# A Mamba and mixture-of-experts kernel: a planner with other durations, scans by quarter, and convolutions as diagonal products

## The chip, the cores and the metric

The kernel runs on one core of one Trainium2 chip, as one launch. The metric is device time in microseconds of that core. A core has five engines that run their own instruction lists and wait for each other through semaphores: TensorE (PE, matrix products into PSUM), VectorE (DVE), ScalarE (ACT), GpSimd (POOL) and SyncE (SP, which here issues DMAs). Everything is float32.

## The reference

Input is `x` of 4 x 256 x 64 x 64: four sequences of 4,096 tokens with 256 channels. Two layers follow, and behind the second a mixture of experts.

Layer 0 is a Mamba block. It projects the tokens, normalises them, projects to 512 + 512 channels, sends the first half through a causal convolution over 4 tokens and a silu, and then through a selective scan with 16 states for each of the 512 channels:

```
xc = sum((xp[:, k:k + L, :] * conv_w[:, k] for k in range(K))) + conv_b
xm = silu(xc)
dt = softplus(dbl[..., :16] @ dt_w.T + dt_b)        # per token and channel
dA = exp(dt_l[..., None] * A)                       # per token, channel, state
h  = dA * h + (dt_l * x_l)[..., None] * B_l[:, None, :]
y  = einsum('bdn,bn->bd', h, C_l)
```

Layer 1 is a Mamba-2 block: a projection, a convolution over 4 tokens on 640 channels (512 for x, 64 for B, 64 for C), a silu, and a scan with one decay per token and head (8 heads of 64 channels, 64 states), with normalisations around it. The experts: each token goes to the best of 8 experts (256 to 1024 to 256 with relu), up to a capacity of 2,560 tokens each, and its result is scaled by the router's probability and added.

## The kernel before, in words

Three phases run one after the other: `mixers` (both layers), `experts`, and `turn` (the transposition of the output). Only `mixers` is touched by the change.

**Chunks and stages.** `mixers` cuts the 4 x 4,096 tokens into 64 chunks of T = 256 tokens. A chunk passes the stages `front0` (layer 0's projections and convolution, L719), `mid0` (dt and u = dt times x, written to DRAM and read back in another layout), `scan` (L831), `tail0`, `front1` (layer 1's projections and convolution), `ssd` (layer 1's scan in matrix form) and `back1` (router and the scatter of rows to the experts). The stages of several chunks run at the same time.

**The scan.** A chunk's scan has 16 units: j (four groups of 128 channels) times f (four groups of states). A tile of 128 partitions by 1,024 elements holds 4 blocks of 256 tokens (32 channels times 4 states on the partitions, four channel groups in the free dimension). In a unit, ACT computes the decays `da` (four exponentials of 255 elements with a scale per partition), DVE multiplies `ub = u * B` into PSUM and runs one `tensor_tensor_scan` over all 1,024 elements, `h = da * h + ub` (L880), POOL multiplies `p = h * C`, and PE adds up the states of `p` with `sum4` into `py`. The first element of each block of `da` is zero, so that the one scan starts each block anew. What comes from the chunk before is put into `ub`'s first elements: POOL and ACT compute `e0 = exp(dt * A) * hlast` once per j (three small instructions), and DVE adds it to four elements per unit (`ub<-ub,e`, the fix-up). `hlast` is the last column of h, copied by ACT. The `da` tiles are three fixed ones.

**The convolutions.** `front0` and `front1` write the pre-convolution values into `raw` (128 x 4 x 259, three tokens of halo in front; one buffer for both layers). `to_taps` (L684) writes it to DRAM, and `tapped` (L690) reads it back for each j with four DMAs, one for each tap, each shifted by a token, so that the partitions hold 4 taps x 32 channels. `convolve` (L700) makes four products with 32 output rows each, whose weights `taps_m` and `taps_x` (L524) are 128 x 32: PE adds up the four taps. ACT adds the bias. The B and C channels of layer 1 (`rbc`) already use four products with diagonal 128 x 128 weights, straight from SBUF.

**The order of the work.** Nothing in `mixers` is issued at once. Each operation goes into a `Plan` with its engine, an estimated duration (`mm`, `transpose`, `act`, `copy`, `dve`, `gps`, `dma`, from L219), its dependencies and a slot: `at` (L712) sets the slot to the chunk's number times 16 plus a stage offset (FRONT0, MID0, TAIL, SSD, BACK) plus, before, an entry of the table SHIFT for the n-th call. `order` (L284) then plays the engines through: whenever an engine is free, it takes the ready operation with the lowest slot that has room in its tile rings, where a value reaches another engine SIGNAL = 0.15 us late. The starts of this play give the order in which the instructions are written out; on the chip each engine runs its list in that order. All planned operations carry the line L378, where `issue` emits them; they are told apart by their tiles. A product `p` is marked `ride`: the planner starts it beside a scan, since DVE's scan (one input in PSUM) leaves free what POOL and DVE's operations with two SBUF inputs share, and ties it behind the DVE operation in front of the scan.

Of the kernel before, what the change touches and what calls it, by code (L numbers as in the profile page):

```python
# [20 lines left out]
P = 128  # L21
T = 256
# [21 lines left out]
TAIL, SSD, BACK = 18, 29, 37  # L44
AHEAD = 4

SHIFT = {
    1: -2.3, 4: 1.4, 5: 0.2, 6: -1.3, 7: -0.3, 8: -0.3, 9: -0.3, 10: -0.3, 11: -0.3, 12: -0.3, 14: -0.3, 15: -0.3,
    16: -0.3, 17: -0.3, 18: -0.3, 19: -0.3, 20: -0.3, 21: -0.3, 22: -0.3, 23: -0.3, 24: -0.3, 25: -0.3, 26: -3.3,
    27: -2.2, 28: 0.2, 29: -0.1, 30: -2.2, 31: -2.2, 32: -2.2, 33: -2.2, 34: -2.2, 35: -2.2, 36: -2.2, 37: 1.2,  # L50
    38: 0.5, 39: -2.2, 40: -2.1, 41: -2.2, 42: -2.7, 43: -2.2, 44: -2.2, 45: -6.0, 46: -2.2, 47: -2.2, 48: -2.2,
    49: -2.2, 50: -2.2, 51: -2.2, 52: -9.4, 53: -2.2, 54: -1.4, 55: -2.2, 56: -2.2, 57: -2.2, 58: -2.2, 59: -2.2,
    60: -4.7, 61: -2.2, 62: -2.2, 63: -2.2, 64: -2.2, 65: -2.2, 66: -2.2, 67: -2.7, 68: -2.2, 69: -2.2, 70: -2.2,
    71: -0.1, 72: -2.2, 73: -2.2, 74: -2.2, 75: -5.9, 76: -4.8, 77: -2.2, 78: -2.2, 79: -2.7, 80: -2.2, 81: -2.2,
    82: -2.2, 83: -2.2, 84: -2.2, 85: -5.2, 86: -2.2, 87: -2.2, 88: -2.2, 89: -2.2, 90: -2.2, 91: -1.4, 92: -2.2,
    93: -2.2, 94: -2.2, 95: -2.7, 96: -2.2, 97: -2.2, 98: -2.2, 99: -2.2, 100: -2.2, 101: -2.2, 102: -2.2,
    103: -2.2, 104: -2.2, 105: -2.2, 106: -2.3, 107: -4.0, 108: -2.0, 109: -2.2, 110: -2.2, 111: -2.2, 112: -2.2,
    113: -1.8, 114: -1.3, 115: 0.9, 116: -0.3, 117: 1.8, 118: -0.3, 119: 0.1, 120: -0.3, 121: -0.3, 123: -0.3,
    124: -0.3, 125: -0.3, 126: 0.6, 127: -1.2, 128: -0.3, 129: -0.3, 130: 0.3, 131: 0.4, 132: -1.4, 133: -0.3,
    134: -0.3, 135: -0.3, 136: 1.6, 137: -0.3, 140: 0.6,  # L60
}
# [88 lines left out]
class Plan:  # L150
# [6 lines left out]
    SIGNAL = 0.15  # L157
# [61 lines left out]
    def mm(self, out, left, right, **kw):  # L219
        rows, n = out.shape[0], self.width(right)  # L220
        w = max(0.24, n / 550) if rows > 64 else max(0.16, n / 900) if rows > 32 else max(0.15, n / 1500)
        self.note("PE", w, self.nc.tensor.matmul, (out, left, right), kw, (out,), (left, right), join=out.root)

    def transpose(self, out, src, ident):
        w = 0.08 + 0.1 * src.shape[0] / P
        self.note("PE", w, self.nc.tensor.transpose, (out, src, ident), {}, (out,), (src,), join=out.root)

    def act(self, out, src, func, **kw):
        w = 0.2 + self.width(out) / 1200
        self.note("ACT", w, self.nc.scalar.activation, (out, src, func), kw, (out,), (src, *kw.values()))  # L230

    def copy(self, out, src):
        self.note("ACT", 0.2 + self.width(out) / 1200, self.nc.scalar.copy, (out, src), {}, (out,), (src,))
# [7 lines left out]
    def dve(self, name, *args, **kw):  # L241
        out, *rest = (*args, *kw.values())
        tensors = [a for a in rest if isinstance(a, Part) or hasattr(a, "ap")]
        n = max(self.width(a) for a in (out, *tensors))
        port = len([a for a in tensors if self.on_sbuf(a) and self.width(a) > 1]) > 1
        if name == "tensor_tensor_scan":
            n, port = 2 * n, False
        op = self.note("DVE", 0.14 + n / 960, getattr(self.nc.vector, name), args, kw, (out,), rest, port=port)
        op.scan = name == "tensor_tensor_scan"
        if op.scan:  # L250
            self.scans.append(op)

# [3 lines left out]
    def gps(self, name, *args, ride=False, **kw):  # L256
        w = 0.3 + self.width(args[0]) * 2.02e-3
        f = getattr(self.nc.gpsimd, name)
        self.note("POOL", w, f, args, kw, (args[0],), args[1:], port=True, ride=ride)
# [7 lines left out]
    def scatter(self, out, rows, src, bound):  # L267


        def f(out, rows, src):  # L270
            return self.nc.gpsimd.indirect_dma_start(
                out=out,
                out_offset=bass.IndirectOffsetOnAxis(ap=rows, axis=0),
                in_=src,
                in_offset=None,
                bounds_check=bound,
                oob_is_err=False,
            )

        self.note("POOL", 1.8, f, (out, rows, src), {}, (out,), (rows, src), lag=4.0)  # L280
# [3 lines left out]
    def order(self):  # L284
# [16 lines left out]
        for op in self.ops:  # L301
            if not op.missing:
                heappush(waiting[op.engine], (0.0, op.seq, op))
        done = 0
        scan = before = last = shared = None

        def room(op, now):
            for root in op.roots:
                if not root.begun:
                    ring, queue = rings.setdefault(root.ring, []), queues[root.ring]  # L310
                    ring[:] = [o for o in ring if o.left or o.until + self.SIGNAL > now]
# [6 lines left out]
        while done < len(self.ops):  # L318
# [6 lines left out]
            for e in engines:  # L325
# [3 lines left out]
                if free[e] > now:  # L329
                    continue  # L330
# [17 lines left out]
                heappush(events, free[e])  # L348
                if op.port:
                    port[e] = free[e]  # L350
# [7 lines left out]
                for root in op.roots:  # L358
                    root.left -= 1
                    root.until = max(root.until, op.end)  # L360
                    if not root.left:
                        heappush(events, root.until + self.SIGNAL)
                for u in op.users:
                    u.missing -= 1
                    late = op.end if u.engine == e and not op.lag else op.end + self.SIGNAL
# [23 lines left out]
def tile_conv_attn_hybrid(ctx: ExitStack, tc: tile.TileContext, a: dict, out: bass.AP, cap: int, st: int):  # L389
# [41 lines left out]
    def mixers(es):  # L431
# [92 lines left out]
        def taps(scales, name):  # L524

            t = wp.tile([P, NG, R], F32, name=name, tag=name)
            for g in range(NG):
                nc.gpsimd.tensor_scalar(t[:, g], sum4, scales[:, g : g + 1], None, ALU.mult)
            return t

        taps_m = taps(m_cw, "taps_m")
        taps_x = taps(s_cw, "taps_x")

# [118 lines left out]
        def silus(*tiles, gates=0):  # L652
# [5 lines left out]
            r.acts(sum(0.2 + Plan.width(t) / 1200 for t in tiles) / len(calls) + 2.6 / len(calls), calls)  # L658
# [25 lines left out]
        def to_taps(raw, tag):  # L684

            d = scratch([NG, R, TAPS - 1 + T], tag)
            r.dma("SP", spread_rows(d), raw)
            return d

        def tapped(d, j):  # L690
            t = work([P, SQ, T], "raw4", 3)
            for k in range(TAPS):
                r.dma(
                    "SP",
                    t[k * R : (k + 1) * R],
                    d[j * SQ : (j + 1) * SQ, :, k : k + T].rearrange("g c l -> c g l"),
                )
            return t

        def convolve(raw4, weights, j, dst, bias, get):  # L700
            pi = get(T)
            for i in range(SQ):
                r.mm(pi[i * R : (i + 1) * R], weights[:, j * SQ + i], raw4[:, i], start=True, stop=True)
            r.act(dst, pi, AF.Identity, bias=bias[:, j : j + 1])
# [14 lines left out]
        def front0(k_):  # L719
# [28 lines left out]
            for half in range(2):  # L748
# [13 lines left out]
                if half == 0:  # L762
                    keep(raw, "raw0")
                    d = to_taps(raw, "raw0_d")
            for j in range(KD):
                k_.at(FRONT0 + 5 + j)
                part = tapped(d, j)
                k_.at(FRONT0 + 7 + j)
                convolve(part, taps_m, j, pre0[:, KC + KD + j], m_cb, bank_a)
# [51 lines left out]
        da_bufs = []  # L821
        for i in range(3):
            t = wp.tile([P, SQ, T], F32, name=f"da{i}", tag=f"da{i}")
            nc.gpsimd.memset(t[:, :, 0:1], 0.0)
            da_bufs.append(t)
        turn = iter(range(10**9))

        def decay_tile():
            return r.tile(lambda: da_bufs[next(turn) % len(da_bufs)], [P, SQ, T], "da", len(da_bufs))

        def scan(k_):  # L831
# [10 lines left out]
            for j in range(KD):  # L842
# [17 lines left out]
                k_.at(j * SQ - 1)  # L860
                if later:

                    e0 = work([P, SQ, SQ], "e0", 2)
                    r.gps("tensor_tensor", e0, neg_a0[:, sl], dt4[:, :, 0:1].to_broadcast([P, SQ, SQ]), ALU.mult)
                    r.act(e0, e0, AF.Exp)
                    r.gps("tensor_tensor", e0, e0, k_.prev.hlast[:, sl], ALU.mult)
                for f in range(SQ):
# [3 lines left out]
                    da = decay_tile()  # L871
                    for q in range(SQ):
                        r.act(da[:, q, 1:], dt4[:, q, 1:], AF.Exp, scale=neg_a0[:, j * SQ + q, f : f + 1])
# [3 lines left out]
                    if later:  # L877
                        r.tt(ub[:, :, 0], ub[:, :, 0], e0[:, :, f], ALU.add)
                    h = work([P, SQ, T], "h", 3)
                    r.dve("tensor_tensor_scan", h.flat(), da.flat(), ub.flat(), 0.0, ALU.mult, ALU.add)  # L880
# [50 lines left out]
        def front1(k_):  # L931
# [56 lines left out]
            d = to_taps(raw, "raw1_d")  # L988
# [46 lines left out]
            for j in range(KD):  # L1035
                k_.at(TAIL + 6 + j)
                part = tapped(d, j)
                k_.at(TAIL + 7 + j)
                convolve(part, taps_x, j, pre1[:, KD + j], s_cb, bank_b)
# [402 lines left out]
def layouts(i):  # L1442
# [14 lines left out]
    def by_tap(w):  # L1457

        return np.asarray(w).reshape(NG, R, TAPS).transpose(2, 1, 0).reshape(P, NG)
# [73 lines left out]
```

## Time and profile before

| | us |
|---|---|
| median of three runs | 6952.74 (6948.43 to 6954.37) |
| the profiled execution | 6966.12 |
| its span, first to last instruction | 6964.3 |
| first scan starts, last scan starts | 109.4, 5725.2 |
| DVE busy | 5670.3 (81%) |
| PE busy | 6084.7 (87%) |
| ACT busy | 4892.5 (70%) |
| POOL busy | 3431.0 (49%) |

The mean granted PE clock is 0.906 of full speed. In the page's rows of slices each digit stands for one fortieth of the span and gives tenths of busy time; PEclk is the granted clock in tenths. A row of groups reads: line, engine, operation, output<-inputs, shapes, count, busy time, mean ns of one, and the idle time of the engine in front of it with what ended it. PE shows each float32 product as two records. A row of the timeline reads: start, duration, engine, line, operation, tiles, shapes, count. DVE and PE take up an instruction before the one in front of it has ended, so that starts, and not durations, tell what an instruction costs in a dense sequence. A row of the table of stretches gives the length, then busy time and count of PE, weight loads, DVE, ACT and POOL, the granted clock, the DMA share and GB/s.

### The profile page before, as it was taken

The numbers are of one execution on the slowest core, as the hardware profiler recorded it, in microseconds if no ns is written. First come the engines' busy times: TensorE is split into PE (matmuls) and PEld (weight loads), VectorE is DVE, ScalarE is ACT, GpSimd is POOL, SyncE is SP. The second block draws the span as 40 slices with busy tenths as digits, with TensorE's granted clock in tenths as the row PEclk, the third lists the DMA queues.
The fourth block names the chain that finished last, engine by engine and source line by source line (L and its number), as shares of the span: only waits on it lengthen the run. The fifth ranks groups of instructions, "written<-read, shape, count | busy, mean of one in ns | idle before, by whom it ended". The sixth has DMA issues, their size and how long they took to land. (4 is left out here: it accounts for less than half of the span.)

```text
span 6964.3 us, 114017 instructions
## 1 busy us (share of the span) xinstructions
PE 6084.7 (87%) x37672; PEld 4128.5 (59%) x37672; DVE 5670.3 (81%) x7646; ACT 4892.5 (70%) x12007; POOL 3431.0 (49%) x2632
## 2 busy tenths in 40 slices
PE   5788888888888888888888888888888877999996
PEld 3455555555555555555555555555555546888886
DVE  4899999999999999999999999999999983434443
ACT  4778888888887778788887777878777863333332
POOL 3455555555555555555555555555555552333331
PEclk7899999999888988998898888989888888999998
DMA  6966667666666666666666666666666633555556
GB/s 178 255 172 178 181 178 182 178 178 178 178 177 173 174 172 176 174 176 171 174 178 177 175 178 176 179 177 176 171 175 176 174 106 132 189 194 197 193 191 238
DMA packets 1125137, 1245.56 MB, mean 179 GB/s; under 512 B 111888, under 2 KB 1093652, under 8 KB 1115330
## 3 DMA queue, kind: packets, MB, share of 16 engines
q1 hardware_dynamic: 1083458, 1008.76, 54.9%
q0 software_dynamic: 30000, 210.98, 8.5%
q10 hardware_dynamic: 11088, 18.53, 0.7%
q8 instruction: 299, 4.90, 0.3%
q14 instruction: 292, 2.39, 0.1%
HBM read 919.92 MB, written 311.63 MB: 177 GB/s over the span
## 5 line engine op out<-in xcount | busy, mean ns | idle before, releaser
L378 POOL TENSOR_TENSOR p<-h,bc 128x1024 f32<-128x1024 f32 x1024 | 2420.7, 2364 | 1980.3 <-DVE ub L378 1371.8
L378 DVE TENSOR_TENSOR_SCAN h<-da,ub 128x1024 f32<-128x1024 f32 x1024 | 2341.8, 2287 | 190.5 <-ACT da L378 69.1
L378 ACT ACTIVATE da<-dt,w_m_Alog 128x255 f32<-128x255 f32 x4096 | 1791.1, 500 | 26.1 <-DVE h L378 17.6
L378 DVE TENSOR_TENSOR ub<-u,bc 128x1024 f32<-128x1024 f32 x1024 | 1370.2, 1338 | 23.9 <-DMA dt<-dt_d 11.5
L378 PE MATMUL py<-p,sum 128*32 128x256 f32 x8192 | 719.0, 434 | 255.2 <-POOL p L378 242.9
L378 PE MATMUL b<-t,w_W_in 128*128 128x256 f32 x2304 | 640.2, 424 | 17.6 <-DVE res L378 10.5
L378 ACT COPY hlast<-h 128x4 f32<-128x4 f32 x1024 | 198.7, 194 | 598.7 <-DVE h L378 596.8
L378 PEld LDWEIGHTS py<-p,sum 128*32 128x32 f32 x8192 | 182.0, 114 | 693.9 <-POOL p L378 399.4
L378 PEld LDWEIGHTS b<-t,w_W_in 128*128 128x128 f32 x2304 | 458.7, 208 | 163.8 <-issue 44.2
L378 PE MATMUL a<-t,w_m_in_w 128*128 128x256 f32 x2048 | 549.8, 422 | 3.5 <-DVE t L378 3.5
L1381 PE MATMUL ph<-xt,w 128*128 128x256 f32 x2272 | 517.1, 381 | 11.5 <-DMA w<-in_w_exp_dram,w_at 6.4
L378 PEld LDWEIGHTS a<-t,w_m_in_w 128*128 128x128 f32 x2048 | 415.9, 211 | 149.5 <-issue 61.0
L1392 PE MATMUL po<-w,hid 128*128 128x256 f32 x2272 | 502.0, 379 | 0.0
L1381 PEld LDWEIGHTS ph<-xt,w 128*128 128x128 f32 x2272 | 427.3, 191 | 70.4 <-ACT hid L1383 7.3
L1392 PEld LDWEIGHTS po<-w,hid 128*128 128x128 f32 x2272 | 431.7, 190 | 58.7
L378 PE MATMUL a<-raw,taps_m 128*32 128x256 f32 x2048 | 211.3, 492 | 234.1 <-DMA raw<-raw_d 169.9
L378 PE MATMUL c<-cum,after 128*128 128x512 f32 x512 | 325.7, 724 | 96.8 <-DVE ex L378 89.9
L1358 DVE CAST number<-rows 128x2 uint32<-128x2 f32 x71 | 12.0, 170 | 476.1 <-DMA tok_d<-fixed,number 461.4
L1356 ACT ACTIVATE tn<-rows 128x256 f32<-128x256 f32 x142 | 82.5, 597 | 414.0 <-DMA rows<-buf_d,row_at 413.5
L1404 POOL DMA_INDIRECT tok_d<-fixed,number x142 | 145.9, 1028 | 390.0 <-DVE fixed L1402 307.6
L378 ACT ACTIVATE cum<-upto,da 128x128 f32<-128x128 f32 x1024 | 337.4, 396 | 0.0
L378 ACT ACT_TABLE_LOAD x256 | 328.4, 1283 | 4.5
(237 smaller groups left out, 11087.4 us busy)
## 6 DMA issues: line engine op xcount, KB each, us to landing
raw<-raw_d SPq DMA_DIRECT2D x2048, 128.0 KB
dt<-dt_d SPq DMA_DIRECT2D x1024, 128.0 KB
u<-u_d SPq DMA_DIRECT2D x1024, 128.0 KB
raw_d<-raw SPq DMA_DIRECT2D x128, 518.0 KB
gx_d<-pre SPq DMA_DIRECT2D x64, 1024.0 KB
bc<-bc_d SPq DMA_DIRECT2D x1024, 64.0 KB
gx<-gx_d SPq DMA_DIRECT2D x256, 256.0 KB
dt_d<-mid SPq DMA_DIRECT2D x64, 512.0 KB
```

The costliest lines, as they stand in the source:

```text
L378: op.issued = f(*map(placed, args), **{k: placed(v) for k, v in kw.items()})
L1356: act(tn[:, j], rows[:, j, TOK:], AF.Identity, scale=rows[:, j, 1:2], bias=rows[:, j, 2:3])
L1358: nc.vector.tensor_copy(number, rows[:, :, 3])
L1381: mm(ph, w1[:, k, f * P : (f + 1) * P], xt[:, k], start=k == 0, stop=k == KC - 1)
L1392: mm(po[:, j], hid[:, f, j * P : (j + 1) * P], w2[:, f], start=f == 0, stop=f == KF - 1)
L1404: nc.gpsimd.indirect_dma_start(out=tok_d, out_offset=bass.IndirectOffsetOnAxis(ap=number[:, j : j + 1], axis=0), in_=fixed[:, j], in_offse ...
```

## The change

- **The planner.** SHIFT is empty. The durations of matrix products, transpositions, ACT, DVE and POOL operations are other numbers; SIGNAL is a value per engine, and BEHIND a second one for a dependent operation on the same engine. At most LANES = 8 DMAs of SP are under way at once in the plan. TAIL, SSD and BACK are one slot later.
- **The scan.** One scan of 1,024 elements becomes four of 256, one for each block, each with its own first state: the column of `hlast` of the chunk before, as a per-partition operand (0.0 in a sequence's first chunk). The computation of `e0`, the fix-up of `ub` and the zeros in `da` go; `da` is computed for 256 elements per block.
- **The convolutions.** `to_taps` and `tapped` go, and with them the DRAM copy of `raw` and 34 DMAs per chunk (2 writes and 32 reads). `convolve` makes four accumulating products with diagonal 128 x 128 weights per j, on `raw` shifted by the tap. `taps_m` and `taps_x` become 16 diagonals each, made by POOL in the set-up.

```diff
-TAIL, SSD, BACK = 18, 29, 37
+TAIL, SSD, BACK = 19, 30, 38
...
-SHIFT = {
...
-}
+SHIFT = {}
...
-    SIGNAL = 0.15
+    SIGNAL = {"DVE": 0.13, "ACT": 0.19, "PE": 0.21, "POOL": 0.12}
+    BEHIND = {"DVE": 0.13, "ACT": 0.14, "PE": 0.0, "POOL": 0.13}
+    LANES = 8
...
-        w = max(0.24, n / 550) if rows > 64 else max(0.16, n / 900) if rows > 32 else max(0.15, n / 1500)
+        w = max(0.224, n / 592) if rows > 64 else max(0.12, n / 1100) if rows > 32 else max(0.15, n / 1500)
...
-        w = 0.2 + self.width(out) / 1200
+        aps = sum(isinstance(v, Part) or hasattr(v, "ap") for v in kw.values())
+        w = 0.06 + self.width(out) / 1130 + 0.09 * aps
...
+    def scans_of(self, out, a, b, starts):
+
+        key, f = object(), self.nc.vector.tensor_tensor_scan
+        for i, start in enumerate(starts):
+            args = (out[:, i], a[:, i], b[:, i], start, ALU.mult, ALU.add)
+            w = 0.07 + self.width(out[:, i]) / 480
+            op = self.note("DVE", w, f, args, {}, (out[:, i],), (a[:, i], b[:, i], start), join=key)
+        op.scan = True
+        self.scans.append(op)
...
-        w = 0.3 + self.width(args[0]) * 2.02e-3
+        w = 0.15 + self.width(args[0]) * 2.1e-3
...
-        taps_m = taps(m_cw, "taps_m")
-        taps_x = taps(s_cw, "taps_x")
+        taps_m, taps_x = (diagonal(w, n) for w, n in ((m_cw, "taps_m"), (s_cw, "taps_x")))
...
-        def convolve(raw4, weights, j, dst, bias, get):
-            pi = get(T)
-            for i in range(SQ):
-                r.mm(pi[i * R : (i + 1) * R], weights[:, j * SQ + i], raw4[:, i], start=True, stop=True)
+        def convolve(raw, weights, j, dst, bias, get):
+            pi = get(T)
+            for k in range(TAPS):
+                r.mm(pi, weights[:, j * TAPS + k], raw[:, j, k : k + T], start=k == 0, stop=k == TAPS - 1)
             r.act(dst, pi, AF.Identity, bias=bias[:, j : j + 1])
...
-                if later:
-
-                    e0 = work([P, SQ, SQ], "e0", 2)
-                    r.gps("tensor_tensor", e0, neg_a0[:, sl], dt4[:, :, 0:1].to_broadcast([P, SQ, SQ]), ALU.mult)
-                    r.act(e0, e0, AF.Exp)
-                    r.gps("tensor_tensor", e0, e0, k_.prev.hlast[:, sl], ALU.mult)
...
-                    da = decay_tile()
+                    da = work([P, SQ, T], "da", 3)
                     for q in range(SQ):
-                        r.act(da[:, q, 1:], dt4[:, q, 1:], AF.Exp, scale=neg_a0[:, j * SQ + q, f : f + 1])
+                        r.act(da[:, q], dt4[:, q], AF.Exp, scale=neg_a0[:, j * SQ + q, f : f + 1])
...
-                    if later:
-                        r.tt(ub[:, :, 0], ub[:, :, 0], e0[:, :, f], ALU.add)
                     h = work([P, SQ, T], "h", 3)
-                    r.dve("tensor_tensor_scan", h.flat(), da.flat(), ub.flat(), 0.0, ALU.mult, ALU.add)
+                    r.scans_of(h, da, ub, [k_.prev.hlast[:, j * SQ + q, f : f + 1] if later else 0.0 for q in range(SQ)])
```

`diagonal` (L508) is the helper that made the B and C weights before; it writes `ident` times a column of scales for each of the n columns.

## The prediction

> **What bounds the kernel now.** I read the page's busy shares and slices first, then the groups, then DVE and PE in order of time. The page's chain that ended last covers about 1% of the span (the output at the end), so it says nothing of the first 5,700 us.
>
> ```profile
> PE 6084.7 (87%) x37672; PEld 4128.5 (59%) x37672; DVE 5670.3 (81%) x7646; ACT 4892.5 (70%) x12007; POOL 3431.0 (49%) x2632
> ...
> DVE  4899999999999999999999999999999983434443
> ...
> PEclk7899999999888988998898888989888888999998
> ...
> L378 DVE TENSOR_TENSOR_SCAN h<-da,ub 128x1024 f32<-128x1024 f32 x1024 | 2341.8, 2287 | 190.5 <-ACT da L378 69.1
> ...
> L378 PE MATMUL a<-raw,taps_m 128*32 128x256 f32 x2048 | 211.3, 492 | 234.1 <-DMA raw<-raw_d 169.9
> ```
>
> DVE is over nine tenths busy in every slice of the mixer stage (slices 3 to 33); the experts behind it are untouched by the diff. From 1000 to 5000 us there are 728 scans: 4000/728 = 5.494 us a scan unit, 87.9 us a chunk of 16 units; 64 chunks make 5,626 us. So everything is a question of the 87.9 us. Of a chunk DVE waits 4.0 us for others (its named waits between 2000 and 3000 us are 45 us, for 11.4 chunks). PE is close behind:
>
> ```profile
> 2000.00:3000.00 1000.00, 880.95 (x5731) 559.08 (x5733) 922.55 (x1191) 799.60 (x1984) 543.38 (x392) 0.90 0.66 175
> ```
>
> In this table of stretches PE is busy 881 of 1000 us, DVE 923, and the granted clock is 0.90. In order of time, DVE:
>
> ```profile
> 156.59 1.22 DVE L378 TENSOR_TENSOR ub<-u,bc 128x1024 f32<-128x1024 f32 x1
> 157.92 2.29 DVE L378 TENSOR_TENSOR_SCAN h<-da,ub 128x1024 f32<-128x1024 f32 x1
> 160.24 1.23 DVE L378 TENSOR_TENSOR ub<-u,bc 128x1024 f32<-128x1024 f32 x1
> ...
> 3005.10 1.23 DVE L378 TENSOR_TENSOR ub<-u,bc 128x1024 f32<-128x1024 f32 x1
> 3006.36 0.17 DVE L378 TENSOR_TENSOR ub<-ub,e 128x4 f32<-128x4 f32 x1
> 3006.66 2.29 DVE L378 TENSOR_TENSOR_SCAN h<-da,ub 128x1024 f32<-128x1024 f32 x1
> 3008.86 0.39 DVE L378 TENSOR_TENSOR state<-state,c 128x256 f32<-128x256 f32 x1
> ```
>
> Durations overlap, so I use start-to-start. [...] A dependent successor waits longer: ub to scan 1.33 (first chunk, no fix-up), ub to fix-up to scan 1.26 + 0.29 = 1.55.
>
> **The change on DVE, per chunk.** Four parts.
> (a) The fix-up goes. Before, 13 of 16 units have ub and fix-up adjacent and 3 something between: 13 x 1.55 + 3 x (1.13 + 0.29) = 24.4 us. In the changed kernel's instruction order 4 units have ub directly before the scans and 12 other work between: 4 x 1.33 + 12 x 1.13 = 18.9. That is -5.5; about six of the twelve fillers are too short (0.08 us) for the 0.2 us wait, +0.6; the four first chunks never had a fix-up: -4.7.
> (b) One scan becomes four of 256 elements, each 0.533 us and an overhead. [...] But the first state is now a per-partition operand. The nearest row with one and a PSUM source is this:
>
> ```profile
> 2067.27 0.48 DVE L378 SCALAR_TENSOR_TENSOR row<-c,rr,res 128x264 f32<-128x264 f32 x1
> 2067.66 0.17 DVE L378 BATCH_NORM_AGGREGATE mv<-stats 128x2 f32<-128x6 f32 x1
> ```
>
> 0.39 us start-to-start for 264 elements (0.275): overhead 0.116. Four scans 2.60 against 2.20: +0.40, with 15/16 of the chunks +6.2. [...] I take +6.2. [...]
> (c) POOL shares a path with DVE's two-SBUF-input operations: ub's mean is 1.345 between 1000 and 5000 us, against 1.22 undisturbed, 2.0 a chunk. Of 25.9 us of such overruns between 2000 and 3000 us, 11.3 stand beside POOL's e operations, which go (-1.0); the others are late p products, which longer scans cover better: 0 to -1.0. I take -1.5.
> (d) DVE's small operations cost 0.20 us behind the one they depend on and 0.07 otherwise. Pairs of neighbours outside the scan units fall from 42 to 33 a chunk: 9 x 0.12 = -1.1.
> Named waits (4.0 us): a planner fed with other durations may take all of them or add as much; no row prices it. I take a quarter off, -1.1. Sum: -4.7 + 6.2 - 1.5 - 1.1 - 1.1 = -2.2, so 85.7 us.
>
> **The change on PE, per chunk.** Here the change costs most:
>
> ```profile
> 3001.57 0.64 PE L378 MATMUL a<-raw,taps_m 128*32 128x256 f32 x8
> 3002.14 3.72 PE L378 MATMUL b<-g,w_m_out_w 128*128 128x256 f32 x16
> 3005.80 0.65 PE L378 MATMUL c<-xdt,bt 128*64 128x256 f32 x4
> ```
>
> Each product is two records. Eight 32-row records take 0.57 us, four column groups running beside each other; a full 128 x 128 product takes 3.66/16 = 0.228 a record (the B and C convolution, already four diagonal products, has 0.228 too). Eight convolutions of 8 records cost 4.3 us warm; as 64 full records 64 x 0.228 = 14.6, +10.3. Adding PE's groups with the median spacings of 2000 to 3000 us gives 70.9 us a chunk; PE really occupies 78.0, and 70.9/78.0 = 0.91 is the granted clock. After: 81.2 warm. At clock 0.90 that is 90 us, over DVE's 85.7, so the change rests on the clock:
>
> ```profile
> 3074.00:3076.00 2.00, 1.96 (x20) 0.35 (x12) 1.97 (x2) 1.98 (x3) 2.00 (x2) 1.00 0.41 118
> 3076.00:3078.00 2.00, 0.00 (x0) 0.00 (x0) 1.83 (x3) 1.99 (x7) 1.66 (x2) 0.97 0.90 241
> 3078.00:3080.00 2.00, 0.51 (x8) 0.23 (x8) 1.97 (x2) 2.00 (x6) 2.00 (x2) 0.50 0.66 173
> ```
>
> After about 4 us without matmuls the clock is 0.50, and stays so for some 12 us; the experts, PE 99% busy from 6000 to 6500 us, run at 1.00. PE now idles 10.5 us a chunk (119 us in that 1000). The waits for the taps' loads (170 us on PE and 36 on the weight loads over the run, 3.2 a chunk, up to 5.8 us each) go, and PE has more to do in the rest. I take clock 0.97: 83.7 us, and 2 us of waits, 85.7: even with DVE. [...]
>
> **Edits that I cost at nothing.** SP loses 34 of 92 issues a chunk (2 writes, 32 loads of 0.43 us) and its wait for raw; DVE's named waits for loads are under 1 us in 1000, so on DVE this gives 0. ACT loses four small exponentials a chunk (0.8 us) and does 256 instead of 255 elements; it is 80% busy. POOL's two e operations per quarter (220 us in all) are counted in (c). There is one raw buffer for both layers, held now until the last tap product: the next layer's halo copy and ACT's writes queue behind it. ACT's 0.47 us per block and a semaphore stand before PE's next convolution, 0 to 2.4 us a chunk, inside PE's 2 us of waits. Set-up: 32 diagonals at 0.62 instead of 0.37 us put POOL's halo memset 8 us later, at 48 us, still ahead of ACT's first raw write at 53. The first chunk's trip (raw done at 56, last convolution at 72.1) becomes 8 records x 4 x 0.24 behind the z half at 58.5: -5.5. The last stages start one slot later: up to +5, mostly under other work, +1.
>
> **Sum.** 64 x -2.2 = -141, -5.5 and +1: -145. The profiled execution took 6966.1 us (span 6964.3), so it would take 6821; the median of the runs is 13.4 lower, 6952.7, and gives **6807**.
>
> **The rivals.**
> [...]
> C, slower: PE becomes the bound because the clock stays low. With waits of 3.1 us PE needs 81.2/clock + 3.1, which passes 87.9 at a clock below 0.958. At 0.93 it is 90.4: 64 x 2.5 - 5 = **7108**. For it: 0.90 today, and PE's queue is in order, so one late p or ex (up to 9.3 and 5.8 us) stops all. Against: the raw waits go, and the experts' 1.00.
> D, no change: the gain on DVE is eaten by its waits for PE (g, xdt, gm), 4.0 becoming 6.2: **6950**.
>
> **How the numbers follow.** Likeliest, A, 0.58, its own range 6700 to 6930; B 0.22; C 0.15; D 0.05. Faster by over 0.2% (14 us, about what this measurement can tell): A and B, 0.80; within: 0.05; slower: C, 0.15. The range 6590 to 7000 leaves out B's lowest 0.05 and 0.11 of C.
>
> **What would show it.** Right: four 256-element scans start 0.65 us apart (B: 0.60); no fix-up; ub near 1.22; PEclk at 0.95 or more; the conv records at 0.228; 85 to 86 us a chunk. Wrong: PE 97% busy at clock 0.92 with DVE's named waits grown (C), or scans 0.70 apart.

## The result, and the profile after

The changed kernel takes 6862.84 us (median of four runs, 6858.16 to 6865.77); the kernel before, run beside it, 6953.25. The ratio is 0.9871 with a 95% interval of 0.9854 to 0.9888: 1.3% faster, 90 us where 145 were forecast. The profiled span went from 6964.3 to 6863.9 us, and the first scan starts at 103.4 us instead of 109.4.

The page of the changed kernel, busy shares, slices and the groups that answer to those shown of before:

```profile
PE 6323.1 (92%) x37672; PEld 4654.0 (68%) x37672; DVE 5764.5 (84%) x9758; ACT 4840.3 (71%) x11767; POOL 3154.7 (46%) x2149
...
DVE  4999999999999999999999999999999983444343
...
PEclk8999999999999999999999999999999998999998
...
L381 DVE TENSOR_TENSOR_SCAN h<-da,hlast,ub 128x256 f32<-128x256 f32 x3840 | 2548.3, 725 | 38.8 <-DVE red L381 0.8
...
L381 PE MATMUL a<-raw,taps_m 128*128 128x256 f32 x2048 | 525.5, 408 | 114.5 <-ACT pre L381 114.5
```

DVE stays at nine tenths or more through the mixer stage. PEclk is 9 in every slice of it but the first (mean of the whole span 0.977, before 0.906). The scans are four times as many and last 725 ns each with the operand, and the convolution's idle time is no longer put down to a load of `raw` but to ACT's `pre`. The table of stretches, same columns as before:

```profile
2000.00:3000.00 1000.00, 934.35 (x5866) 662.41 (x5869) 955.69 (x1605) 805.68 (x1984) 494.11 (x308) 0.99 0.42 119
```

PE is now busy for 934 of 1000 us and the clock is 0.99; the DMA share fell from 0.66 to 0.42. In order of time, on DVE, a group of scans in a sequence's first chunk (first state 0.0) and one with the state in `hlast`:

```profile
108.52 2.42 DVE L381 TENSOR_TENSOR_SCAN h<-da,ub 128x256 f32<-128x256 f32 x4
110.97 1.23 DVE L381 TENSOR_TENSOR ub<-u,bc 128x1024 f32<-128x1024 f32 x1
...
2159.05 2.66 DVE L381 TENSOR_TENSOR_SCAN h<-da,hlast,ub 128x256 f32<-128x256 f32 x4
2161.74 1.23 DVE L381 TENSOR_TENSOR ub<-u,bc 128x1024 f32<-128x1024 f32 x1
```

The timeline counts four scans in a row as one entry. Its length less the last scan's own (664 and 725 ns) leaves three starts: (2.42 - 0.664)/3 = 0.585 us from start to start with a constant, (2.66 - 0.725)/3 = 0.645 us with the operand. On PE, a convolution and what follows it:

```profile
2161.69 1.99 PE L381 MATMUL a<-raw,taps_m 128*128 128x256 f32 x8
2163.52 0.60 PE L381 MATMUL c<-ident,pre 128*128 128x128 f32 x4
```

Eight full records take 1.83 us, 0.229 each.

From 1000 to 5000 us there are 2955 scans of 256 elements, so a chunk of 64 takes 4000 x 64/2955 = 86.63 us, against 87.91 before. All periods below are counted in this way, which is good to about 0.1 us. 64 chunks x 1.28 are 82 us, and 6 are the earlier first scan: together 88 of the 90.

The period that was forecast is 85.7 us. That is not far off, but not yet a reason: the change has three parts, and each could have given or taken any share of it.

### The profile page after: what moved, and what is told of

Read it like the earlier page. It is cut to its first block, busy times and chain, and to the rows that moved or that the text cites. A ratio compares the mean times of both kernels' runs of the same rounds, so it can differ in the third digit from the quotient of the medians.

```text
span 6863.9 us, 111155 instructions
## 1 busy us (share of the span) xinstructions
PE 6323.1 (92%) x37672; PEld 4654.0 (68%) x37672; DVE 5764.5 (84%) x9758; ACT 4840.3 (71%) x11767; POOL 3154.7 (46%) x2149
## 5 line engine op out<-in xcount | busy, mean ns | idle before, releaser
L381 POOL TENSOR_TENSOR p<-h,bc 128x1024 f32<-128x1024 f32 x1024 | 2477.3, 2419 | 2514.6 <-DVE mid L381 578.4
L381 DVE TENSOR_TENSOR_SCAN h<-da,hlast,ub 128x256 f32<-128x256 f32 x3840 | 2548.3, 725 | 38.8 <-DVE red L381 0.8
L381 ACT ACTIVATE da<-dt,w_m_Alog 128x256 f32<-128x256 f32 x4096 | 1851.1, 504 | 0.5 <-issue 0.5
L381 DVE TENSOR_TENSOR ub<-u,bc 128x1024 f32<-128x1024 f32 x1024 | 1294.0, 1264 | 15.8 <-DMA u<-u_d 6.8
L381 PE MATMUL py<-p,sum 128*32 128x256 f32 x8192 | 631.9, 394 | 51.8 <-POOL p L381 40.9
L381 PE MATMUL a<-raw,taps_m 128*128 128x256 f32 x2048 | 525.5, 408 | 114.5 <-ACT pre L381 114.5
L381 PEld LDWEIGHTS a<-raw,taps_m 128*128 128x128 f32 x2048 | 396.0, 200 | 232.1 <-ACT pre L381 144.2
L381 PE MATMUL b<-raw,taps_x 128*128 128x256 f32 x2048 | 504.0, 388 | 26.9 <-ACT pre L381 23.0
L381 PEld LDWEIGHTS b<-raw,taps_x 128*128 128x128 f32 x2048 | 371.8, 189 | 159.3 <-ACT pre L381 90.9
L381 PE MATMUL a<-t,w_m_in_w 128*128 128x256 f32 x2048 | 475.3, 386 | 4.4 <-DVE t L381 3.8
L1312 ACT ACTIVATE tn<-rows 128x256 f32<-128x256 f32 x142 | 81.2, 596 | 424.3 <-DMA rows<-buf_d,row_at 424.0
```

Source lines behind the costliest of these rows:

```text
L381: op.issued = f(*map(placed, args), **{k: placed(v) for k, v in kw.items()})
L1312: act(tn[:, j], rows[:, j, TOK:], AF.Identity, scale=rows[:, j, 1:2], bias=rows[:, j, 2:3])
```

## The experiments

Each run is compared with the kernel before on the same chip; the interval is the 95% one of that ratio.

### Which part of the change gives the time

**One scan of 1,024 elements back, with its fix-up; the planner and the convolutions as changed.**

```diff
-                    da = work([P, SQ, T], "da", 3)
+                    da = decay_tile()
...
+                    if later:
+                        r.tt(ub[:, :, 0], ub[:, :, 0], e0[:, :, f], ALU.add)
-                    r.scans_of(h, da, ub, [k_.prev.hlast[:, j * SQ + q, f : f + 1] if later else 0.0 for q in range(SQ)])
+                    r.dve("tensor_tensor_scan", h.flat(), da.flat(), ub.flat(), 0.0, ALU.mult, ALU.add)
```

> The changed kernel with the scan part undone: one scan of 1,024 elements, the e operations and the fix-up, under the new planner and with the new convolutions. Theory A (DVE sets the pace and the four scans cost more than the fix-up they replace, once the planner puts other work into the fix-up's waits): the scans lose 5.2 us a chunk again, the fix-up costs some 2.3 and the e operations 1.0 on the shared path, so -1.9 us a chunk, about 6740 us. Rival B (the four scans are where the gain comes from): the chunk grows by the 6.8 us that ub and fix-up lost, less 5.2, so about 6950 us. Rival C (PE sets the pace): 6860 us, within 20.

Measured: 6782.4 us, ratio 0.9748 (0.9732 to 0.9764), 85.22 us a chunk. Without the four scans the kernel is 80 us faster than with them, so the four scans are not where the gain comes from.

**The convolutions through DRAM back; the planner and the four scans as changed.**

```diff
-        taps_m, taps_x = (diagonal(w, n) for w, n in ((m_cw, "taps_m"), (s_cw, "taps_x")))
+        taps_m = taps(m_cw, "taps_m")
+        taps_x = taps(s_cw, "taps_x")
...
-                convolve(raw, taps_m, j, pre0[:, KC + KD + j], m_cb, bank_a)
+                part = tapped(d, j)
+                convolve(part, taps_m, j, pre0[:, KC + KD + j], m_cb, bank_a)
```

> The changed kernel with the convolution part undone: 32-row products on taps read back from DRAM, under the new planner and with the four scans. Theory A (DVE sets the pace, the convolutions are beside its path): 6830 to 6890 us, PE's clock back near 0.9 with little effect. Rival B (the gain comes from the convolutions, through the clock and the freed DMA queue): 6940 us or more. Rival C (PE sets the pace of the changed kernel): faster, 6750 us or less, since PE has 9 us a chunk less to do.

Measured: 6736.25 us, ratio 0.9685 (0.9669 to 0.9701), 84.21 us a chunk. It beats both kernels: the convolutions straight from SBUF cost 127 us here, although the first scan starts 5 us later without them (108.7 us). This is the number of the theory that PE sets the pace; the held runs below take that up.

**Both back: only the planner is as changed.** The edit is the two above together.

> Both parts undone: only the planner's durations, latencies and lanes, the empty SHIFT and the later slots are left. Theory A: DVE's small chains (-1.1 us a chunk), part of the fix-up's waits and of the named waits go: -2 to -3 us a chunk, 6760 to 6820 us. Rival B (the planner alone brings nothing; the two other parts do): 6940 to 7050 us.

Measured: 6783.3 us, ratio 0.9751 (0.9733 to 0.9769), 85.33 us a chunk. The planner alone gives 170 us, nearly twice what the whole change gives.

**The kernel before, with SHIFT emptied and the three stage slots one later; its old durations stay.**

```diff
-TAIL, SSD, BACK = 18, 29, 37
+TAIL, SSD, BACK = 19, 30, 38
...
-SHIFT = {
...
-}
+SHIFT = {}
```

> The kernel before with only SHIFT emptied and the last stages a slot later; old durations and SIGNAL. Theory A (the other durations and latencies carry the planner's gain of 170 us): 6930 to 7050 us. Rival B (the dropped SHIFT and the later slots carry it): 6780 to 6830 us.

Measured: 6789.3 us, ratio 0.976 (0.974 to 0.9781). The durations from traces, the new SIGNAL, BEHIND and LANES are worth no more than the 6 us between this run and the one before, once the table is empty and the slots are later.

**The kernel before, with SHIFT emptied and nothing else.**

```diff
-SHIFT = {
...
-}
+SHIFT = {}
```

> The kernel before with the table SHIFT emptied and nothing else changed (the old durations and the old stage slots 18, 29 and 37 stay). Theory A, the table of shifts held the time up: 6780 to 6800 us, as with later slots. Theory B, the later slots did it: 6930 to 6970 us.

Measured: 6956.5 us, ratio 1.0012 (1.0002 to 1.0023), 88.03 us a chunk. Emptying the table alone gives nothing, so with the table empty it is the later slots that give the time. Named waits of DVE between 1000 and 5000 us are 140.5 us in this run and 48.6 us with the later slots, 3.1 and 1.0 us a chunk: two of the 3.3 us by which the chunks differ (88.03 and 84.77). The later slots with the old table were not run, and neither was each of the three slots alone.

The first three and the changed kernel together, with the planner alone as the base:

| | convolutions through DRAM | convolutions from SBUF |
|---|---|---|
| one scan, fix-up | 6783.3 | 6782.4 |
| four scans | 6736.25 | 6862.84 |

From SBUF the convolutions cost nothing beside one scan and 127 us beside four; four scans gain 47 us beside the old convolutions and lose 80 beside the new. Neither part has a price of its own.

### What the first state costs

**First states 0.0 in every chunk.** What one chunk leaves to the next is not computed.

```diff
-                    r.scans_of(h, da, ub, [k_.prev.hlast[:, j * SQ + q, f : f + 1] if later else 0.0 for q in range(SQ)])
+                    r.scans_of(h, da, ub, [0.0 for q in range(SQ)])
```

> The changed kernel with 0.0 as first state of all scans in place of the column of hlast; this leaves out what comes from the chunk before. Theory A (DVE sets the pace): the operand costs 0.06 us a scan, 3.6 us a chunk; PE stands at 81 us a chunk plus its waits and takes back some of it: 6630 to 6710 us. Rival C (PE sets the pace): 6830 to 6863 us.

Measured: 6765.4 us, ratio 0.9728 (0.9711 to 0.9744), 85.36 us a chunk, between the two forecasts. The groups between 1000 and 5000 us of this run:

```profile
L381 DVE TENSOR_TENSOR_SCAN h<-da,ub 128x256 f32<-128x256 f32 x2999 | 1809.8, 665 | 29.3 <-DVE dest L381 0.4 <-DVE red L381 0.4
L381 DVE TENSOR_TENSOR ub<-u,bc 128x1024 f32<-128x1024 f32 x749 | 1023.5, 1367 | 6.6
```

Each scan lasts 665 instead of 725 ns, so the operand is 0.06 us; with 60 of a chunk's 64 scans on the average (a sequence's first chunk has none), 3.6 us a chunk. Only 1.27 of it comes back. The `ub` products last 1367 instead of 1260 ns (the changed kernel's row is below), 16 x 0.107 = 1.7 us a chunk: nearly half of what is freed is taken by longer products. The order is planned anew here, without the dependence on `hlast`.

### Is it TensorE or VectorE that sets the pace of the changed kernel?

**Half of the convolutions' products, planned anew.**

```diff
-            for k in range(TAPS):
-                r.mm(pi, weights[:, j * TAPS + k], raw[:, j, k : k + T], start=k == 0, stop=k == TAPS - 1)
+            for k in range(2, TAPS):
+                r.mm(pi, weights[:, j * TAPS + k], raw[:, j, k : k + T], start=k == 2, stop=k == TAPS - 1)
```

> The changed kernel with only the last two of the four taps in both 512-channel convolutions; this leaves out half of their computation. PE has 7.2 us a chunk less to do, with as many PSUM banks handed to ACT and back and the same single raw buffer. Theory A (PE's array time sets the pace of the changed kernel together with DVE): 6710 to 6780 us, as with the convolutions undone (6736). Rival B (the handing over of banks, or the raw buffer that is held longer, costs the time): 6820 to 6865 us.

Measured: 6797.7 us, ratio 0.9771 (0.9751 to 0.9791), between the two forecasts. But a planner that sees fewer products writes another order, so this run changes two things. The next one keeps the order.

**Half of the products, in the changed kernel's own order.** The planner still counts all four, and only the issuing is left out.

```diff
             for k in range(TAPS):
+                r.ghost = k < 2
-                r.mm(pi, weights[:, j * TAPS + k], raw[:, j, k : k + T], start=k == 0, stop=k == TAPS - 1)
+                r.mm(pi, weights[:, j * TAPS + k], raw[:, j, k : k + T], start=k == 2, stop=k == TAPS - 1)
```

> The changed kernel in its own order (the planner still plans four taps, and every other instruction keeps its place on its engine), with the first two of the four diagonal products of each convolution left out. Half of each convolution is not computed. TensorE has about 7.2 us less per chunk and nothing else changes. Theory A, TensorE's time is on the path that sets the chunk (its handovers to VectorE end late because its array is full): about half of it comes back, 3.6 us in each of some 53 chunks, 6650 to 6720 us. Theory B, the array has slack and it is the order that costs: 6830 to 6863 us.

Measured: 6835.3 us, ratio 0.9836 (0.9819 to 0.9852), 86.34 us a chunk. PE's busy time falls from 80.9 to 75.3 us a chunk (3736 and 3489 us in 4000), and 0.29 us of it comes back. So PE's computing time is not what sets the pace in this order. PE's named waits between 1000 and 5000 us (who waited, for whom; total us, times, longest), of the changed kernel:

```profile
PE a L381 <- ACT pre L381: 89.1, 46, 2.2
PE b L381 <- ACT bcs L381: 49.9, 47, 1.1
...
PE py L381 <- POOL p L381: 1.9, 6, 0.4
```

and of this run:

```profile
PE py L385 <- POOL p L385: 99.4, 125, 1.3
PE a L385 <- ACT pre L385: 68.9, 46, 1.9
PE c L385 <- DVE xdt L385: 66.3, 45, 1.5
PE c L385 <- DVE gm L385: 51.9, 46, 1.9
```

What PE no longer computes it waits for: for `xdt` and `gm` from DVE and `p` from POOL, for which it had hardly waited. DVE's waits for PE's `c` bank hardly move, 65.4 and 40.7 us in the changed kernel and here:

```profile
DVE xdt L385 <- PE c L385: 59.6, 51, 1.2
DVE state L385 <- PE c L385: 40.6, 46, 0.9
```

**Two DVE passes and one ACT addition less, planned anew.** Layer 0's softplus is computed as ln(e + 1) without the correction of the rounding of e + 1, a mathematically equal form.

```diff
-            r.act(w, e, AF.Identity, bias=one_c)
-            r.dve("scalar_tensor_tensor", e, w, -1.0, e, ALU.add, ALU.subtract)
-            r.act(w, w, AF.Ln)
-            r.tt(dt, dt, e, ALU.subtract)
+            r.act(w, e, AF.Ln, bias=one_c)
```

> The changed kernel with layer 0's softplus as relu + ln(1 + e), without the two DVE passes (stt and tensor_tensor over 1,024 elements, 1.2 and 1.1 us) that correct the rounding of 1 + e, and without ACT's addition of 1. DVE has 2.3 us a chunk less to do, PE the same. Theory A (PE sets the pace with DVE): it comes through by a third or less, 6800 to 6860 us. Rival B (DVE alone sets the pace): 64 x 2.3, 6700 to 6740 us.

Measured: 6798.9 us, ratio 0.9776 (0.9755 to 0.9797).

**The same three instructions not issued, in the changed kernel's own order** (marked as in the held run above).

```diff
+            r.ghost = True
             r.act(w, e, AF.Identity, bias=one_c)
...
             r.dve("scalar_tensor_tensor", e, w, -1.0, e, ALU.add, ALU.subtract)
...
-            r.act(w, w, AF.Ln)
+            r.ghost = False
+            r.note("ACT", 0.06 + Plan.width(w) / 1130, nc.scalar.activation, (w, e, AF.Ln), {"bias": one_c}, (w,), (w,))
+            r.ghost = True
             r.tt(dt, dt, e, ALU.subtract)
+            r.ghost = False
```

> The changed kernel in its own order, with the two VectorE passes and the one ScalarE addition that correct the rounding in layer 0's softplus not issued (the product's own rounding stays; a mathematically equal form). VectorE has about 2.3 us less per chunk and every other instruction keeps its place. Theory A, TensorE paces the chunk and VectorE waits for it: the time freed turns into waits, 6830 to 6863 us. Theory B, VectorE still paces the chunk: 2.3 us in each of some 53 chunks and a little in the prologue come back, 6715 to 6745 us.

Measured: 6762.84 us, ratio 0.9732 (0.9716 to 0.9748), 85.42 us a chunk, 1.21 us shorter. By starts, the two DVE instructions left out took 2.2 us a chunk. DVE's work falls by another 0.5, mostly because `xdt<-xdt,dend` lasts 680 ns instead of 1097 (why it lasted so long is told further down). That row, and DVE's named waits:

```profile
L385 DVE TENSOR_TENSOR xdt<-xdt,dend 128x512 f32<-128x512 f32 x94 | 63.9, 680 | 110.3 <-PE c L385 110.3
...
DVE xdt L385 <- PE c L385: 115.9, 65, 2.3
DVE state L385 <- PE c L385: 55.0, 47, 1.2
DVE pre L385 <- PE c L385: 15.4, 47, 0.3
```

Against 65.4 and 40.7 us in the changed kernel, DVE waits longer for PE's `c` bank; all its named waits go from 138.3 to 209.2 us in 4000, 1.5 us a chunk, which is over half of the 2.7 that were freed. So in the changed kernel's order a microsecond left out on DVE is worth about half of one (1.21 of 2.2), a microsecond less on PE 0.05 (0.29 of 5.6). Of the two it is DVE, with its handovers to and from PE, that sets the pace. ACT was not tested alone: it is busy for 81% of these 4000 us, and its addition of 1, left out in the same run, made about 0.5 us a chunk.

### The better version, and how much the order alone moves

**The convolutions through DRAM, with the shorter softplus, planned anew.** It joins the edits of the second run and of the softplus.

> The same on the kernel with the convolutions undone (6736 us, where DVE waits 1.1 us a chunk). Theory A (there DVE alone sets the pace): 64 x 2.3 = 147 less, 6570 to 6630 us. Rival B (another engine is as close): 6680 us or more.

Measured: 6756.0 us, ratio 0.9706 (0.9685 to 0.9727), 84.88 us a chunk: with less work on DVE it is no faster than the run without the shorter softplus (0.9669 to 0.9701).

**The same work in the order of the second run:** the convolutions through DRAM, and the softplus's three instructions planned and not issued, as above.

> The changed kernel with the convolutions of the kernel before, in the order of the run that had them (6736 us), and with the same three instructions of layer 0's softplus not issued. There VectorE waited 1.1 us per chunk. Theory A, VectorE alone paces that kernel: 2.3 us in each of some 53 chunks come back, 6590 to 6630 us. Theory B, another engine or the order is as close behind there: 6700 us or more.

Measured: 6719.43 us, ratio 0.9671 (0.9655 to 0.9687), the lowest of all, but its interval overlaps that of the same order with the longer softplus. A chunk takes 84.18 us against 84.21. The passes left out took 2.1 us of DVE a chunk and the chunk is no shorter; its named waits rise from 55.6 to 135.9 us in 4000. The largest waits of this run:

```profile
DVE xdt L385 <- PE c L385: 38.4, 47, 1.2
DVE ex L385 <- PE c L385: 25.8, 48, 0.5
DVE row L385 <- PE c L385: 24.1, 47, 0.5
DVE pre L385 <- PE c L385: 15.4, 47, 0.3
```

Here the passes were worth nothing in the chunk, so DVE's work alone no longer sets the pace of that order. What does was not settled: PE is busy for 88% of these 4000 us, and ACT for 82%.

Three pairs have the same work in two orders, planned anew and held: the ratios are 0.9771 and 0.9836 (half of the products), 0.9776 and 0.9732 (shorter softplus), 0.9706 and 0.9671 (with the convolutions through DRAM too). By 6953 us they are 45, 31 and 24 us apart (the last hardly clear of the noise), and the planner's order for what is really issued wins only the first. A part that moves no more than this in a re-planned kernel can't be told from a redrawn order; so the 47 us of the four scans can't.

The 127 us of the convolutions are not clear of it either. The two kernels with an empty table differ in nothing but three slots, so in nothing but the order, and are 167 us apart (6956.5 and 6789.3). And with the shorter softplus the kernels with the convolutions from SBUF and through DRAM are only 43 us apart, planned anew (6798.9 and 6756.0) as well as held (6762.84 and 6719.43). So the convolutions cost 127, 43 or 0 us, by what stands beside them.

## Why the prediction was right, and where it was not

The time forecast was 6807, and 6863 came, with the case that was forecast: the clock rose, the fix-up went, and the period fell a little. Of its signs, 86.63 us a chunk lies outside the 85 to 86; the scans (0.645 us apart), PEclk and the convolution's records came as said. But with the new planner the scans and the convolutions together lost time, and the gain is that of the new order, as the runs show: that the number came so near is in part luck. By its steps:

| a chunk, us | forecast | measured |
|---|---|---|
| (a) fix-up and `ub` in front of it | -4.7 | -5.2 |
| (b) four scans for one | +6.2 | +5.75 |
| (c) products beside POOL's | -1.5 | +0.1 |
| (d) small operations and all others | -1.1 | -1.4 |
| named waits of DVE | -1.1 | -0.6 |
| period | -2.2 | -1.3 |

The measured terms come from starts on DVE between 1000 and 5000 us, each less the named wait in front of the next start, for a chunk of 64 (before 16) scans.

**Steps (a) and (d)** came out near the forecast. (a) is the fix-up's 4.2 us and 2.3 us of `ub`, less the 1.36 that belong to (c). The 1.13 us that (a) sets for a `ub` with other work behind it stand in the trace before: a `ub` starts at 3009.97, the `xdt<-c,dt` behind it at 3011.10 and the next at 3011.70, so 1,024 elements take 1.13 us and 512 take 0.60. But more than half of (a) is not owed to the fix-up's end. With the planner alone, fix-up still there, the fix-up takes 2.35 us a chunk by starts instead of 4.2, and `ub` 20.7 instead of 22.0. DVE's idle time in front of the scans shows the same, before and with the planner alone (1000 to 5000 us):

```profile
L378 DVE TENSOR_TENSOR_SCAN h<-da,ub 128x1024 f32<-128x1024 f32 x728 | 1664.8, 2287 | 135.4 <-ACT da L378 48.1 <-POOL p L378 4.2 <-DVE ub L378 1.8
...
L381 DVE TENSOR_TENSOR_SCAN h<-da,ub 128x1024 f32<-128x1024 f32 x750 | 1711.0, 2281 | 34.7 <-DVE ub L381 0.5 <-ACT pre L381 0.5 <-POOL rbc L381 0.3
```

In an order that fills the fix-up's waits with other work, dropping it frees less on DVE than the four scans cost there (with the new convolutions 4.2 and 5.6 us, by starts).

**Step (b)** was right in its cause and 0.45 us too dear. No run shows the 0.533 us that the sum sets for the 256 elements of a scan. What the runs show are whole scans, from start to start: 2.20 us for 1,024 elements (3006.66 to 3008.86 before), and for 256 elements 0.585 with a constant and 0.645 with the operand. As an estimate from the two lengths with a constant, 256 elements take 256 x (2.20 - 0.585)/768 = 0.54 us; that leaves 0.05 of a scan with a constant and 0.11 of one with the operand. The 0.116 read off the row with an operand and a PSUM source came near that: by the 1.13 and 0.60 us above, its 264 elements would take 264 x 0.53/512 = 0.27 of its 0.39 us, again an estimate, which leaves 0.12. Four scans start over 2.58 us with the operand, where 2.60 were forecast, and over 2.34 without. So the overhead depends on the operand. Rival B (cheap first states) is excluded by the same number: the operand costs 0.06 us.

**Step (c)** failed. It took the collisions beside POOL's `e` operations as gone and saw only `ub`. The groups of DVE operations between 1000 and 5000 us, before:

```profile
L378 DVE TENSOR_TENSOR ub<-u,bc 128x1024 f32<-128x1024 f32 x727 | 977.5, 1345 | 5.4 <-DMA u<-u_d 0.4 <-DMA xtail<-in_x_dram 0.3
L378 DVE TENSOR_TENSOR decay<-decay,gm 128x1024 f32<-128x1024 f32 x91 | 116.7, 1282 | 0.0
...
L378 DVE TENSOR_TENSOR xdt<-xdt,dend 128x512 f32<-128x512 f32 x91 | 61.0, 670 | 0.0
```

and after:

```profile
L381 DVE TENSOR_TENSOR ub<-u,bc 128x1024 f32<-128x1024 f32 x738 | 930.2, 1260 | 6.3
L381 DVE TENSOR_TENSOR decay<-decay,gm 128x1024 f32<-128x1024 f32 x92 | 144.0, 1565 | 0.0
...
L381 DVE TENSOR_TENSOR xdt<-xdt,dend 128x512 f32<-128x512 f32 x92 | 100.9, 1097 | 57.0 <-PE c L381 57.0
```

`ub` is 85 ns shorter, 16 x 0.085 = 1.36 us a chunk. But the two `decay` products of a chunk are 283 ns longer and the two `xdt<-xdt,dend` 427 ns: 2 x 0.71 = 1.42, and 1.43 by their starts. The means mix two kinds: 46 of the 92 `xdt<-xdt,dend` meet a `p` that began before them and last 1529 ns, the others 666. The collisions moved, and nothing is left of the 1.5.

**Waits.** "A quarter off" was a little too much, and hid that they are others. DVE's three largest between 1000 and 5000 us before:

```profile
DVE h L378 <- ACT da L378: 48.1, 44, 1.4
DVE g L378 <- PE py L378: 31.3, 30, 2.0
DVE xdt L378 <- PE c L378: 27.5, 30, 1.8
```

and after:

```profile
DVE xdt L381 <- PE c L381: 65.4, 67, 1.2
DVE state L381 <- PE c L381: 40.7, 46, 0.9
DVE stats L381 <- PE b L381: 17.4, 45, 1.6
```

The sum goes from 163.7 to 138.3 us, 3.6 and 3.0 a chunk. The waits for ACT's `da` and for `py` went; those for PE's `b` and `c` banks took their place.

**PE and the clock.** 81.2 us of warm work were forecast (eight times the row's 0.57 are 4.6 and not 4.3, which takes 0.3 off), 80.9 busy at clock 0.99 were found, with 5.5 us of named waits instead of 2. A record of the convolution takes 0.229 us, forecast 0.228. Eight records take 1.83 us as full products, where eight of 32 rows had taken 0.57, a factor of 3.2. Rival C (a clock below 0.958) is excluded, and which part raised the clock is shown by two runs. One scan with the convolutions from SBUF, and then four scans with those through DRAM, 1000 to 5000 us:

```profile
1000.00:5000.00 4000.00, 3802.90 (x23834) 2671.43 (x23833) 3770.92 (x4968) 3327.29 (x8245) 2314.04 (x1620) 0.99 0.40 120
```
```profile
1000.00:5000.00 4000.00, 3535.64 (x24054) 2247.39 (x24056) 3905.78 (x6599) 3326.07 (x8161) 2059.30 (x1288) 0.95 0.72 184
```

0.99 and 0.95 (over the whole runs 0.974 and 0.943, and 0.923 with both undone): the clock follows the convolutions. One reading behind the step was off: the clock did not need "about 4 us without matmuls". In the rows shown the last product starts before 3076, and the mean of 0.97 from 3076 to 3078 puts the fall to 0.50 at the end of that stretch, some 2 us into the pause.

**The step that was wrong**, besides (c), is the one that put PE "even with DVE", so that the convolutions would cost nothing on DVE. PE was not even: in the held order, half of the products are worth 0.29 us a chunk. And yet the kernel with the convolutions from SBUF is 127 us behind the one with the old ones beside four scans, 86.63 against 84.21 us a chunk. The groups of the run with the old convolutions show where most of it lies:

```profile
L381 DVE TENSOR_TENSOR ub<-u,bc 128x1024 f32<-128x1024 f32 x760 | 1017.7, 1339 | 1.6
...
L381 DVE TENSOR_TENSOR decay<-decay,gm 128x1024 f32<-128x1024 f32 x94 | 114.0, 1213 | 0.0
L381 DVE TENSOR_TENSOR xdt<-xdt,dend 128x512 f32<-128x512 f32 x94 | 65.1, 692 | 0.0
```

Against the changed kernel, `decay` and `xdt<-xdt,dend` are 352 and 405 ns shorter, 1.5 us a chunk; `ub` is 79 ns longer, 1.26 the other way. DVE's named waits are 55.6 us in 4000 instead of 138.3, 1.17 and 3.00 a chunk, the largest of them these:

```profile
DVE ex L381 <- PE c L381: 25.8, 48, 0.5
DVE cdec L381 <- ACT cdec L381: 12.5, 47, 1.1
```

Together 2.1 of the 2.42 us. A piece of the changed kernel in order of time shows how the two go together (in brackets the wait ahead and who ended it):

```profile
2187.95 0.76 DVE L381 BATCH_NORM_STATS2 stats<-b 128x6 f32<-128x256 f32 x2 [1.57 <-PE b L381]
...
2188.63 0.30 DVE L381 BATCH_NORM_AGGREGATE mv<-stats 128x2 f32<-128x6 f32 x2
2188.85 1.19 DVE L381 SCALAR_TENSOR_TENSOR mid<-mid,mid 128x1024 f32<-128x1024 f32 x1
2188.86 3.41 POOL L381 TENSOR_TENSOR p<-h,bc 128x1024 f32<-128x1024 f32 x1 [4.20 <-DVE mv L381]
...
2189.05 1.16 PE L381 MATMUL c<-pre,diag_d 128*128 128x128 f32 x8
...
2190.14 1.09 PE L381 MATMUL c<-decay,xdt 128*64 128x128 f32 x16
...
2191.28 1.53 DVE L381 TENSOR_TENSOR xdt<-xdt,dend 128x512 f32<-128x512 f32 x1 [1.24 <-PE c L381]
```

DVE waits 1.57 us for a product in bank `b` (one of the longest of these waits: 45 of them make 17.4 us). Its small `mv` then releases two things at once: POOL's `p`, after 4.20 us of idle time, and PE's next products into `c`. The second group of these reads `xdt` and ends 2.3 us after `mv`, so DVE, which overwrites `xdt` next, waits another 1.24 us; and then `xdt<-xdt,dend` meets the late `p`: it starts at 2191.28, `p` ends at 2192.27, and `xdt` ends 0.54 us after that. It takes 1.53 us, where the mean before was 0.67. In the held run with half the products both stay, the waits (3.02 us a chunk) and the long products (1573 and 1099 ns). So these come from the place of the instructions in the queues and not from the time that those products take on PE. Whether the convolutions from SBUF must lead to such an order, or this one is a bad draw, is open: with the table empty the order alone moved more than 127 us (the slots' 167), and with the shorter softplus the same exchange costs 43. That the one `raw` buffer stays taken until the last product was not tested.

**The planner.** Two terms of the forecast belonged to the new order, (d) and the waits, together -2.2 us a chunk. Alone the planner is worth 87.91 - 85.33 = 2.58 us, and all of that came with the emptied table and later slots together. The size was about right, but not the place: in its run DVE's named waits are longer than before (4.05 us a chunk) and the small operations as long, and the gain lies in the fix-up and `ub`. With the old durations and the same slots it lies elsewhere again: the fix-up takes 4.2 us, and the named waits are 1.03. The scans and the convolutions, (a) to (c), were forecast at 0.0 us together, and with the new planner they cost 86.63 - 85.33 = +1.30. That is most of the 0.9 us a chunk by which the forecast was too low, with 0.4 the other way from the planner.

**Prologue.** -5.5 us were forecast; the first scan comes 6.0 us earlier (103.4 after 109.4).

Rival D (the gain eaten by waits for PE) had the right place and not the size: those waits are the largest that are left, and they came in place of others and not on top.

## What to carry to other kernels

A change that also feeds an automatic order must be taken apart before its parts are judged: the part in the title (scans, convolutions) lost 80 us and three stage constants with an emptied table won some 165. To price one instruction in a planned kernel, leave it out while the planner still counts it; planning anew moved the time by 24 to 45 us for the same work, and three slots by 167. An engine at 93% busy is not the bound by that: take work from it in place, and see whether the time comes back or turns into its waits.

## What the runs showed of the hardware

A first state as per-partition operand costs a scan 0.06 us (725 and 665 ns, 0.645 and 0.585 us from start to start), a tenth of a scan of 256 elements.

Products with two SBUF inputs on DVE and on POOL went one behind the other here, not side by side. In the piece above `mid`, two inputs in SBUF and started just before `p`, keeps its 1.19 us and `p` takes 3.41 instead of some 2.36; `xdt`, started while `p` runs, ends 0.54 us after it. So the one that comes late pays. A scan, whose `ub` lies in PSUM, does not take part: in the changed kernel the 591 of `p` between 1000 and 5000 us that lie at least nine tenths beside scans take 2.34 to 2.38 us. A mean of such an instruction mixes those that met another and those that did not.

PE's clock of 0.90 before did not come from how long PE was busy: with 53 us more busy time in 1000 (934 against 881) it runs at 0.99, and with half of the convolutions' products left out in the same order (872 of 1000) still at 0.98. It goes with the form of the convolutions: over the whole of the profiled executions it is 0.91 to 0.95 in the seven kernels that have them through DRAM and 0.96 to 0.98 in the seven that have them from SBUF. The loads of `raw`, for which PE waited up to 5.6 us before, are not the whole of it: with four scans and the old convolutions PE's waits for them fell from 119 to 13.4 us in 4000, and the clock is 0.95. Whether it is other pauses or the narrow products themselves was not tested.
